# Second values spread ahead of the text's values, and other work between the product of y and z and the first maxima that read it

## The chip, the core and the metric

The kernel runs on one core of one Trainium2 chip. TensorE multiplies matrices (PE in the profile, with PEld for its loads of the stationary operand), VectorE (DVE) and ScalarE (ACT) work on the results, GpSimd (POOL) does elementwise work and issues gathers, and SyncE (SP) issues nearly all transfers. Each engine runs its own program in order; semaphores tie them. The metric is the device time of one execution in microseconds, as the median of several runs. All data are float32.

## The reference

Two batches of 2048 rows of 640 numbers (x) attend to a context of 128 tokens of 384 numbers, of which the last 4 are "ca" tokens and the first 124 are text.

```python
query = hidden_states @ Wq
keyt = enc @ Wk
valt = enc @ Wv
hs = _mha(query, keyt, valt)                       # text: 8 heads of 80, 124 keys
ca_q1 = jnp.einsum('btc,th->bch', ca, Wq_ca)
ca_q1 = ca_q1[:, indices, :]                       # 384 distinct rows, repeated to 2048
ca_hs1 = _mha(ca_q1, residual, residual)           # adapter, first attention: keys are x
ca_q2 = ca_hs1 @ Wq
ca_k2 = ca @ Wk_ca
ca_v2 = ca @ Wv_ca
ca_hs2 = _mha(ca_q2, ca_k2, ca_v2)                 # adapter, second attention: 4 keys
out = hs + ca_hs2
out = out @ Wout + b_out
out = out + residual
```

The text's attention is large and regular. The adapter's first attention runs over all 2048 rows of x with only 384 distinct queries, and its second has only four keys.

## The kernel before, in words

**Two kinds of work.** The *adapter* of a batch comes in two stages. In the first, x is taken in four blocks of 512 rows. `yz_block` (L756) multiplies a block's transposed rows with a small matrix `wyz` that holds the queries' four tokens by head and what the second attention's keys make of x (tile `pyz`), and ScalarE copies the two halves with a bias (L775, tile `yz`). `maxima` (L792) then multiplies yz with the ca tokens (tile `s`, L799), six times a block, each time 128 partitions of four banks, and VectorE takes the maximum of each (L806, tile `mx`). The tile `s` has one buffer of four PSUM banks, so each `s` product waits for the maximum of the one before. `y_rows` (L779) turns yz for later (`pt_y`). When the four blocks are through, `less_maxima` (L811) subtracts the maxima from the tokens. In the second stage, `contraction` (L825) multiplies again, ScalarE takes the exponential (tile `ea`), and TensorE contracts it with the turned rows (`acc`); at its end come the second attention with its four keys and its product with the values matrix `w2_sb` (`po2`, stored as o2, from which rows are added to the output by gathers on GpSimd).

The *text* comes in 16 units of two tiles of 128 rows: queries (`pq`, L936), scores (`sc`, L971), softmax on VectorE, ScalarE and GpSimd, a turn of the probabilities over device memory (`eb`, `kept`, `pT`, L1017 to L1039), values (`ph`) and the output product (`po`, L1049 on), which VectorE adds to x (`xo`). Tiles of the text that are ready before o2 is are stored and loaded again later (`early`, `xe`).

**What sets the order.** TensorE's order is the program's order. `TensorInOrder` (L18) keeps each matmul in program order and adds up an estimate of TensorE's time so far, `pe.us`. The main body writes the adapter's stages and fills what lies between them: `weave` (L1171) takes the pieces of a stage one by one, and after each lets `fill.run` issue other pieces until the stage's gap in estimated time is full. `Mix` (L98) chooses that other work from several lists (`Fill`, L66): `own` (the adapter's further stages, loads of x and setup), `text`, and `later`. A piece whose needs are not met is passed over, and where no list has one, `run` returns at once. A `Stage` may need a point in estimated time: `y_rows` may start only 1.0 us after its block's product (L1240, with `yz_at` from L776), and the transposes of a loaded block (`x_turn`, L741) 18 or 24 us after its load was issued. `fill.until` (L122) forces a list on until a stage is done. VectorE, ScalarE, GpSimd and SP serve their instructions in the order in which the scheduler puts them, which follows the program.

In the body, each block's maxima come right after `fill.until(done, ("yzT", b, sb))`, which ends with that block's product (L1269 and L1302).

**The values of the setup.** `setup_values` (L617) is one of the stages of `own`. It makes two things. The text's values: for each batch and half, three accumulating products (`pv`), which `spread` copies in three pieces into `vpad`. And the second values, those of the ca tokens: `by_groups` (tile `pvca`, copied to `vca`), then `groups_turned` (tile `pt_vca`, one transpose and four small products), then four instructions of VectorE that spread it into `blk_v`, and last `by_blocks` (tile `pw`), which multiplies it with the output matrix into `w2_sb`. Each `yield` is a point at which other work may be put in between. Tiles like `pv`, `pt_vca`, `pw`, `pyz` and `pq` share a pool of three PSUM banks in turn (`ps_m`); in the second batch's maxima a fourth bank joins.

Of the kernel before, what the change touches and what calls it, by code (L numbers as in the profile page):

```python
# [19 lines left out]
class TensorInOrder:  # L20
# [6 lines left out]
    def matmul(self, out, lhsT, rhs, **kw):  # L27
        ins = self.tc.nc.tensor.matmul(out, lhsT, rhs, **kw)  # L28
        self.tc.keep_in_program_order(ins)
        n = 1  # L30
        for size in rhs.shape[1:]:
            n *= size
        if min(lhsT.shape[0], lhsT.shape[1]) <= 32:
            self.us += (n / 1.2 + 97) / 2e3
        elif min(lhsT.shape[0], lhsT.shape[1]) <= 64:
            self.us += (n / 1.2 + 54) / 1e3
        else:
            self.us += 2 * max(n / 1.2, 109) / 1e3
# [139 lines left out]
def kernel(  # L178
# [39 lines left out]
    nc = tc.nc  # L218
    pe = TensorInOrder(tc)
    dve = VectorBehind(tc)  # L220
    B, S, H = x.shape
    NTOK, CAD = enc.shape[1], enc.shape[2]
    NK = NTOK - T
    D = H // HEADS
    NCH = H // P
    NCC = CAD // P
    NST = S // P
    NSB = S // 512
    HALF = H // 2
# [23 lines left out]
    matmul = pe.matmul  # L253
# [5 lines left out]
    def mm_tile(name, pool=None):  # L259
        if pool is None:  # L260
            pool = ps_turns[ps_turn[0] % len(ps_turns)]
            ps_turn[0] += 1
        return pool.tile([P, 512], F32, tag="mm", name=name)
# [4 lines left out]
    def evacuate(dst, src):  # L268

        turn[0] += 1  # L270
        if on[0][turn[0] % len(on[0])] == "A":
            nc.scalar.copy(dst, src)  # L272
        else:
            dve.tensor_copy(dst, src)
# [51 lines left out]
    vpad = [const.tile([P, HEADS, VH + 2 * VR], F32, name=f"vpad_{b}") for b in range(B)]  # L326
# [47 lines left out]
    w_c = {}  # L374
# [23 lines left out]
    ctxT = sp.tile([P, NCC, B, NTOK], F32, name="ctxT")  # L398
# [54 lines left out]
    def by_groups(name, rows, w):  # L453

        pg = mm_tile(name)
        for cc in range(NCC):
            for g in range(4):
                matmul(
                    pg[G * g : G * (g + 1), :D2], rows[:, cc, :], w[:, cc, D2 * g : D2 * (g + 1)],
                    start=(cc == 0), stop=(cc == NCC - 1), skip_group_check=True,  # L460
                )
        return pg

    def groups_turned(name, t, n):

        pt = mm_tile(name)
        transpose(pt[:, :P], t[:, :P], ident)
        for g in range(4):
            matmul(
                pt[R * g : R * (g + 1), P : P + n], t[:, P:], ident[:, G * g : G * g + n],  # L470
                start=True, stop=True, skip_group_check=True,
            )
        return pt[:, :P].rearrange("p (c k) -> p c k", c=4), pt[:, P : P + n]

    def by_blocks(name, *products):


        for to, rhs, first in products:
            for c in range(4):
                matmul(  # L480
                    to[G * c : G * (c + 1)], blk[name][:, 0, c, :], rhs(c),
                    start=first, stop=False, skip_group_check=True,
                )
        for to, rhs, _ in products:
            matmul(
                to, blk[name][:, 1].rearrange("p g k -> p (g k)"), rhs(4),
                start=False, stop=True, skip_group_check=True,
            )
# [128 lines left out]
    def setup_values():  # L617


        def spread(dst, src, u):  # L620

            s4 = src.rearrange("p (h d) -> p h d", h=4)
            d4 = dst[:, 4 * u : 4 * u + 4, :]
            evacuate(d4[:, :, :VH], s4[:, :, :VH])
            for j in range(2):
                evacuate(
                    d4.rearrange("p (g j) d -> p g j d", j=2)[
                        :, :, j, VH + VR * j : VH + VR * (j + 1)
                    ],
                    s4.rearrange("p (g j) d -> p g j d", j=2)[:, :, j, VH:],  # L630
                )

        pg = by_groups("pvca", caT, w_c["vca"])[:, :D2].rearrange("p (j d) -> p j d", j=2)
        vca = sp.tile([P, D2], F32, name="vca")
        evacuate(vca[:, :P].rearrange("p (j d) -> p j d", j=2), pg[:, :, :VH])
        evacuate(vca[:, P:].rearrange("p (j d) -> p j d", j=2), pg[:, :, VH:])
        yield
        for b in range(B):
            nc.gpsimd.memset(vpad[b], 0.0)
            for u in range(2):  # L640
                pv = mm_tile(f"pv_{b}_{u}")
                for cc in range(NCC):
                    matmul(
                        pv[:, :HALF],
                        ctxT[:, cc, b, :],
                        w_c["v"][:, cc, u * HALF : (u + 1) * HALF],
                        start=(cc == 0),
                        stop=(cc == NCC - 1),
                    )
                spread(vpad[b][:NK], pv[:NK, :HALF], u)  # L650
                yield
        most, rest = groups_turned("pt_vca", vca, B * T)
        for j in range(2):
            k0 = T * j
            dve.tensor_scalar(
                blk["v"][:, 0, :, : B * 2 * T].rearrange("p c (b k) -> p c b k", b=B)[
                    :, :, :, k0 : k0 + T
                ],
                most[:, :, : B * T].rearrange("p c (b t) -> p c b t", b=B),
                side2[:, j : j + 1], None, ALU.mult,  # L660
            )
        for b in range(B):
            n = 2 * T
            dve.tensor_tensor(
                blk["v"][:, 1, :, n * b : n * (b + 1)].rearrange("p g (j t) -> p g j t", j=2),
                rest[:, T * b : T * (b + 1)].rearrange("p (x y t) -> p x y t", x=1, y=1).to_broadcast(
                    [P, 4, 2, T]
                ),
                eighth.rearrange("p (g j x) -> p g j x", g=4, x=1).to_broadcast([P, 4, 2, T]),
                ALU.mult,  # L670
            )
        yield
        for u in range(2):
            cols = slice(u * HALF, (u + 1) * HALF)
            pw = mm_tile(f"pw2_{u}")[:, :HALF]
            by_blocks("v", (pw, lambda c: wout_sb[:, c, cols], True))
            evacuate(w2_sb[:N2, cols], pw[:N2])
        yield
# [9 lines left out]
    yz_at = {}  # L688
# [103 lines left out]
    def maxima(b, sq, mx, sb, gap):  # L792

        yz = yz_of[b, sb]
        for ct in range(NCC):
            for u in range(2):
                q4 = sq.tile([P, 4, 512], F32, tag="sq", name=f"s1_{b}_{sb}_{ct}_{u}")
                for g in range(4):
                    matmul(  # L799
                        q4[:, g, :],  # L800
                        ca0[G * g : G * (g + 1), u, ct * P : (ct + 1) * P],
                        yz[G * g : G * (g + 1), u, :],
                        start=True,
                        stop=True,
                    )
                dve.tensor_reduce(mx[:, ct, u, :, sb], q4, AX.X, ALU.max)  # L806
                yield gap
                if (ct, u) == (1, 0):
                    done.add(("half", b, sb))

    def less_maxima(b, mx):  # L811

        mt = pools["ea"].tile([P, NCC, 2, P], F32, tag="ea", name=f"mt_{b}")
        nc.gpsimd.memset(mt, 0.0)
        mt_cols = mt.rearrange("p a j (g k) -> p (a j) g k", k=32)[:, :, :, ONE]
        dve.tensor_reduce(mt_cols, mx.rearrange("p a j g s -> p (a j) g s"), AX.X, ALU.max)
        yield 1.0
        for j in range(2):
            pm = mm_tile(f"pm_{b}_{j}")
            for ct in range(NCC):  # L820
                transpose(pm[:, ct * P : (ct + 1) * P], mt[:, ct, j, :], ident)
            dve.tensor_tensor(ca0[:, j, :], ca0[:, j, :], pm[:, :CAD], ALU.subtract)
        yield 1.0
# [347 lines left out]
    def weave(main, fill, least=0.0):  # L1171


        due = 0.0
        for gap in main:
            due = fill.run(max(due + gap, min(gap, least)))
# [88 lines left out]
    fill = Mix(pe, (own, 1), (text, 1))  # L1265
    weave(setup_a2(), fill)
    own.parts[:0] = yz_stages(0, 0)
    for sb in range(NSB):
        fill.until(done, ("yzT", 0, sb))  # L1269
        weave(maxima(0, sq, mx_of[0], sb, 2.3), fill, 2.0)  # L1270
    fill.until(done, ("yz", 0, NSB - 1))
    fill.until(done, "values")
# [17 lines left out]
    fill = Mix(pe, (own, 1), (text, 1), (later, 1))  # L1290
# [9 lines left out]
    )  # L1300
    for sb in range(NSB):
        fill.until(done, ("yzT", 1, sb))  # L1302
        weave(maxima(1, sq, mx_of[1], sb, 4.8), fill, 2.0)
    weave(less_maxima(1, mx_of[1]), fill)
    fill.until(done, ("yz", 1, NSB - 1))
# [41 lines left out]
```

## Time and profile before

| what | value |
|---|---|
| three runs | 754.13, 750.59, 754.28 us; median 754.13 us |
| the profiled execution | 750.76 us |
| its span, first to last instruction | 749.1 us |
| granted clock of TensorE | 1.000 |
| TensorE idle in 0 to 150 us | 4.2 (first load), 2.6 (pw), 1.5 (yz), 1.0 (kpad), 0.2, 0.2 us |
| VectorE busy, 300 to 450 us | 109.6 of 150 us |
| moved by the DMA engines | 96.28 MB, 129 GB/s over the span |

A line of the profile's lists of groups and its timeline names the source line, the engine, the operation, and the tiles as out<-in; L28, L41 and L55 are the helpers through which all matmuls, transposes and most of VectorE's instructions go, so one tells them apart by tiles. One float32 matmul stands as two records. "x12" counts the records that were merged. In square brackets stands the time for which the engine had been idle, and what ended it; "issue" is idle time for which the profile shows no releaser. In the timeline the blocks and batches of a tile are not told apart; the times do that: the first batch's maxima run from 50 to 152 us, its contraction to 310, the second batch's maxima from 313 to 457 and its contraction to 603; after that the text is alone.

### The profile page before, as it was taken

The numbers are of one execution on the slowest core, as the hardware profiler recorded it, in microseconds if no ns is written. First come the engines' busy times: TensorE is split into PE (matmuls) and PEld (weight loads), VectorE is DVE, ScalarE is ACT, GpSimd is POOL, SyncE is SP. The second block draws the span as 40 slices with busy tenths as digits, with TensorE's granted clock in tenths as the row PEclk, the third lists the DMA queues.
The fourth block names the chain that finished last, engine by engine and source line by source line (L and its number), as shares of the span: only waits on it lengthen the run. The fifth ranks groups of instructions, "written<-read, shape, count | busy, mean of one in ns | idle before, by whom it ended". The sixth has DMA issues, their size and how long they took to land.

```text
span 749.1 us, 9397 instructions
## 1 busy us (share of the span) xinstructions
PE 727.0 (97%) x3809; PEld 372.2 (50%) x3809; DVE 373.3 (50%) x507; ACT 193.6 (26%) x239; POOL 133.4 (18%) x184
## 2 busy tenths in 40 slices
PE   7999989999989999999999999999999999999998
PEld 4553423343345446555445554434543556566765
DVE  2155736654264447488669586311440526345631
ACT  2221112033344433221112111443534311011100
POOL 7000000002021013225321221010010012631330
PEclk9999999999999999999999999999999999999999
DMA  9927240002824768298999294310920426985893
GB/s 294 169 40 120 34 38 1 0 1 92 127 96 83 187 106 186 88 244 175 187 268 230 60 201 114 116 41 4 190 61 18 127 91 191 237 219 153 214 245 95
DMA packets 147429, 96.28 MB, mean 129 GB/s; under 512 B 118133, under 2 KB 118965, under 8 KB 145338
## 3 DMA queue, kind: packets, MB, share of 16 engines
q1 hardware_dynamic: 142266, 85.10, 48.4%
q0 software_dynamic: 5120, 10.59, 8.1%
q8 instruction: 30, 0.49, 0.3%
q14 instruction: 13, 0.11, 0.1%
HBM read 63.81 MB, written 31.85 MB: 128 GB/s over the span
## 4 chain that ended last, share of the span: by engine, by line
PE 88%; DVE 5%; DMA 3%; issue 2%; ACT 1%; POOL 0%; SPq 0%; DVEq 0%; ACTq 0%; POOLq 0%
PE pq L28 24%; PE po L28 22%; PE s L28 13%; PE sc L28 10%; PE acc L28 6%; PE ph L28 5%; PE pyz L28 3%; DMA pT<-kept 2%; DVE mx L55 1%; PE pk L28 1%; ACT ea L856 1%; DVE m L55 1%; PE pt_y L41 1%; DVE p L55 1%; DVE xt L55 1%
## 5 line engine op out<-in xcount | busy, mean ns | idle before, releaser
L28 PE MATMUL po<-wout_sb,hsT 128*128 128x320 f32 x640 | 186.4, 438 | 1.5 <-DVE q L55 0.8
L28 PEld LDWEIGHTS po<-wout_sb,hsT 128*128 128x128 f32 x640 | 118.5, 190 | 70.5 <-issue 22.5
L28 PE MATMUL pq<-xt,wq_sb 128*128 128x512 f32 x320 | 151.9, 605 | 0.0
L55 DVE TENSOR_REDUCE mx<-s 128x4 f32<-128x2048 f32 x48 | 109.8, 2289 | 69.8 <-PE s L28 69.8
L856 ACT ACTIVATE ea<-s 128x1536 f32<-128x1536 f32 x64 | 92.7, 1448 | 109.3 <-PE s L28 109.2
L1014 POOL TENSOR_TENSOR p<-p,r 128x992 f32<-128x992 f32 x32 | 61.4, 1957 | 253.3 <-DVE r L55 253.3
L55 DVE TENSOR_TENSOR xo<-xo,po 128x320 f32<-128x320 f32 x64 | 31.0, 484 | 142.8 <-PE po L28 142.2
L28 PE MATMUL sc<-kpad,q 128*128 128x248 f32 x384 | 94.2, 385 | 0.1
L28 PEld LDWEIGHTS pq<-xt,wq_sb 128*128 128x128 f32 x320 | 57.0, 189 | 74.9 <-issue 68.4
L28 PEld LDWEIGHTS sc<-kpad,q 128*128 128x128 f32 x384 | 69.2, 189 | 32.4 <-issue 18.5
L55 DVE TENSOR_REDUCE m<-sc 128x4 f32<-128x496 f32 x64 | 42.2, 665 | 51.5 <-PE sc L28 51.4
L28 PE MATMUL s<-ca,yz 32*128 32x384 f32 x512 | 59.4, 533 | 2.5 <-ACT ea L856 2.5
L272 ACT COPY q<-pq 128x512 f32<-128x512 f32 x29 | 17.0, 585 | 163.5 <-PE pq L28 163.5
L28 PE MATMUL s<-yz,ca 32*128 32x512 f32 x384 | 54.7, 639 | 3.3 <-ACT yz L775 1.5
L999 ACT ACTIVATE p<-p 128x992 f32<-128x992 f32 x32 | 33.0, 1030 | 95.2 <-DVE p L55 92.6
L1109 POOL DMA_INDIRECT xo<-o,query x24 | 37.4, 1560 | 111.4 <-DMA xo<-in_x_dram 51.1
L28 PE MATMUL acc<-ea,y_sb 128*32 128x384 f32 x512 | 54.6, 498 | 0.2 <-ACT ea L856 0.2
L28 PE MATMUL ph<-pT,vpad 128*32 128x256 f32 (+1 forms) x512 | 50.0, 387 | 2.0 <-DVE hsT L55 1.8
L55 DVE TENSOR_TENSOR p<-sc,m 128x496 f32<-128x496 f32 x64 | 42.4, 669 | 1.5
L55 DVE STREAM_TRANSPOSE eb<-p 128x1024 f32<-128x1024 f32 x32 | 38.1, 1223 | 3.6 <-POOL p L1014 3.6
L28 PE MATMUL pq<-xt,wq 128*128 128x512 f32 x80 | 37.8, 601 | 0.0
L55 DVE TENSOR_REDUCE r<-p 128x8 f32<-128x992 f32 (+1 forms) x34 | 37.7, 1111 | 0.2
(142 smaller groups left out, 389.8 us busy)
## 6 DMA issues: line engine op xcount, KB each, us to landing
kept<-eb SPq DMA_DIRECT2D x16, 1024.0 KB, 5.1
pT<-kept SPq DMA_DIRECT2D x64, 256.0 KB, 5.5
xi<-in_x_dram SPq DMA_DIRECT2D x44, 256.0 KB, 5.0
xo<-in_x_dram SPq DMA_DIRECT2D x32, 320.0 KB, 5.6
out_dram<-xo SPq DMA_DIRECT2D x22, 320.0 KB, 3.3
xi<-in_x_dram SPq DMA_DIRECT2D x44, 64.0 KB, 4.8
early<-xo SPq DMA_DIRECT2D x8, 320.0 KB
xe<-early SPq DMA_DIRECT2D x8, 320.0 KB, 7.6
```

What stands on the lines that cost most here:

```text
L28: ins = self.tc.nc.tensor.matmul(out, lhsT, rhs, **kw)
L41: ins = self.tc.nc.tensor.transpose(out, in_, ident)
L55: self.last = getattr(self.tc.nc.vector, name)(*args, **kw).ins
L272: nc.scalar.copy(dst, src)
L856: nc.scalar.activation(e, q4[:, :, :CAD], AF.Exp, scale=SCALE)
L999: nc.scalar.activation(e[:, :, :NK], e[:, :, :NK], AF.Exp, scale=SCALE)
L1014: nc.gpsimd.tensor_tensor(et, et, r.unsqueeze(2).to_broadcast([P, HEADS, NK]), ALU.mult)
L1109: nc.gpsimd.indirect_dma_start(out=t, out_offset=None, in_=o2_of[b], in_offset=bass.IndirectOffsetOnAxis(ap=query[:, st : st + 1], axis=0) ...
```

## The change

In `setup_values` the turn of the second values and their spread into `blk_v` come before the text's values; both are the same instructions as before. In the body, after each block's product of y and z, `fill.run` is called once more, for as long as 1.2 us by the kernel's own count are not yet over since that product. The rest of the program is written as it was; since the fill then has other pieces at hand, what is put between later stages differs too.

```diff
@@ setup_values
         evacuate(vca[:, P:].rearrange("p (j d) -> p j d", j=2), pg[:, :, VH:])
         yield
-        for b in range(B):
-            nc.gpsimd.memset(vpad[b], 0.0)
-            for u in range(2):
-                pv = mm_tile(f"pv_{b}_{u}")
-                for cc in range(NCC):
-                    matmul(
-                        pv[:, :HALF],
-                        ctxT[:, cc, b, :],
-                        w_c["v"][:, cc, u * HALF : (u + 1) * HALF],
-                        start=(cc == 0),
-                        stop=(cc == NCC - 1),
-                    )
-                spread(vpad[b][:NK], pv[:NK, :HALF], u)
-                yield
         most, rest = groups_turned("pt_vca", vca, B * T)
...
                 ALU.mult,
             )
         yield
+        for b in range(B):
+            nc.gpsimd.memset(vpad[b], 0.0)
+            for u in range(2):
+                pv = mm_tile(f"pv_{b}_{u}")
+                for cc in range(NCC):
+                    matmul(
+                        pv[:, :HALF],
+                        ctxT[:, cc, b, :],
+                        w_c["v"][:, cc, u * HALF : (u + 1) * HALF],
+                        start=(cc == 0),
+                        stop=(cc == NCC - 1),
+                    )
+                spread(vpad[b][:NK], pv[:NK, :HALF], u)
+                yield
         for u in range(2):
             cols = slice(u * HALF, (u + 1) * HALF)
             pw = mm_tile(f"pw2_{u}")[:, :HALF]
@@ the first batch's maxima
     for sb in range(NSB):
         fill.until(done, ("yzT", 0, sb))
+        fill.run(yz_at[0, sb] + 1.2 - pe.us)
         weave(maxima(0, sq, mx_of[0], sb, 2.3), fill, 2.0)
@@ the second batch's maxima
     for sb in range(NSB):
         fill.until(done, ("yzT", 1, sb))
+        fill.run(yz_at[1, sb] + 1.2 - pe.us)
         weave(maxima(1, sq, mx_of[1], sb, 4.8), fill, 2.0)
```

## The prediction, made before the changed kernel ran

> **What bounds the kernel now.** I read the page first, then the list of waits of TensorE alone, then the timeline around the longest of them on TensorE and on VectorE, and last the list of what the SP queue issued.
>
> From the page (span, then busy time and share of each engine):
>
> ```profile
> span 749.1 us, 9397 instructions
> PE 727.0 (97%) x3809; PEld 372.2 (50%) x3809; DVE 373.3 (50%) x507; ACT 193.6 (26%) x239; POOL 133.4 (18%) x184
> ```
>
> TensorE is the path: 727.0 of 749.1 us, at a granted clock of 1.00 throughout. No edit of this change adds or removes a matmul, so it can only act on the 22.1 us in which TensorE idles. Who ended that idle time (the longest of the waits of TensorE: total, times, longest):
>
> ```profile
> PE pt_ctx L41 <- DMA ctx_sb<-in_ctx_dram: 4.2, 1, 4.2
> PE pw L28 <- DVE blk_v L55: 2.6, 1, 2.6
> PE s L28 <- ACT ea L856: 2.5, 4, 1.3
> PE ph L28 <- DVE hsT L55: 1.8, 1, 1.8
> PE s L28 <- ACT yz L775: 1.5, 2, 0.8
> ```
>
> 4.2 us is the first load, 2.5 and 1.8 us lie in the two contractions. What the two edits aim at is the wait of pw for blk_v (2.6 us) and the waits of the maxima's s for yz (1.5 us, and 0.82 us at 313.26 us that the profile could name only "issue", but that stands at the same place: s right behind pyz). Together 4.9 us: no forecast from these edits can go much beyond that. The timeline of TensorE in the stretch of the first edit (start, length, engine, line, operation; in brackets the idle time before it):
>
> ```profile
> 84.54 1.02 PE L28 MATMUL pvca<-w_vca,caT 128*32 128x160 f32 x24
> 85.50 1.14 PE L28 MATMUL s<-yz,ca 32*128 32x512 f32 x8
> 86.57 3.50 PE L28 MATMUL pv<-w_v,ctxT 128*128 128x320 f32 x12
> 90.28 1.14 PE L28 MATMUL s<-yz,ca 32*128 32x512 f32 x8 [0.22 <-DVE mx L55]
> 91.35 3.50 PE L28 MATMUL pv<-w_v,ctxT 128*128 128x320 f32 x12
> 94.78 1.14 PE L28 MATMUL s<-yz,ca 32*128 32x512 f32 x8
> 95.85 0.33 PE L41 MATMUL pt_vca<-ident,vca 128*128 128x128 f32 x1
> ...
> 98.96 2.89 PE L28 MATMUL pw<-wout_sb,blk_v 128*32 128x320 f32 x20 [2.60 <-DVE blk_v L55]
> 101.78 3.00 PE L28 MATMUL pyz<-xt,wyz 128*64 128x512 f32 x12
> 105.55 1.14 PE L28 MATMUL s<-yz,ca 32*128 32x512 f32 x8 [0.77 <-ACT yz L775]
> ```
>
> And VectorE, which serves in its program's order:
>
> ```profile
> 95.99 2.29 DVE L55 TENSOR_REDUCE mx<-s 128x4 f32<-128x2048 f32 x1 [2.21 <-PE s L28]
> 98.19 0.40 DVE L55 TENSOR_SCALAR blk_v<-pt_vca,side 128x32 f32<-128x32 f32 x2
> 98.51 0.28 DVE L55 TENSOR_TENSOR blk_v<-pt_vca,eighth 128x32 f32<-128x32 f32 x2
> ```
>
> The reader is to see that blk_v itself costs 0.6 us, but stands behind a maximum of 2.2 us, so that pw comes 2.6 us late.
>
> **Part one: the second values ahead.** Same instructions, moved. No transfer moves with them; the two memsets of vpad keep their place in POOL's order, and ACT's copies theirs. I walk through the new order with the durations above. pvca ends at 85.5, its copies on ACT at 85.98, s ends at 86.57; the turn of vca (0.5 us) then runs to 87.05 and waits for nothing. Two pv groups (3.43) end at 90.5. The maximum of the s before it is done at 90.2 (its row starts at 87.97, after the five transposes of x that start at 84.97), so the 0.22 us wait goes too, and s runs to 91.55. VectorE does blk_v behind that maximum, 90.2 to 90.8. The other pv groups end at 95.0, s at 96.05, and pw starts there instead of at 98.96: blk_v is five us old. pyz then starts at 98.9 instead of 101.78: **2.9 us less**. The cover of blk_v is the second s and the last two pv, 4.5 us on TensorE.
>
> [...] This pool has three banks. Before, the turn of vca was followed only by pw; now the third pv group takes its bank, and the bank is freed not by ACT's 0.55 us copies but by blk_v, behind a maximum. By the row blk_v ends at 90.8 and the third pv comes at 91.55: 0.75 us to spare, cost nothing. [...]
>
> **Part two: 1.2 us of other work after each pyz.** It inserts whatever fits by the kernel's own count. In the first batch's blocks 0 and 1 nothing fits (the next stages are not allowed yet): the new order of TensorE is the old one there, and the 0.77 us at 50.28 stays. In block 2 two matmuls of pq_4 (1.8 us) now stand between pyz and s; yz takes 1.26 us on ACT, so the **0.77 us** go. But the order after it moves too. On VectorE the five transposes of x's fourth block now stand ahead of the maximum of s_2_1_0 and not behind it:
>
> ```profile
> 116.37 3.07 DVE L55 STREAM_TRANSPOSE xt<-xi 128x512 f32<-128x512 f32 x5
> 119.36 2.25 DVE L55 TENSOR_REDUCE mx<-s 128x4 f32<-128x2048 f32 x1
> ```
>
> Summed with these rows from pyz at 98.9: s_2_0_0 103.65, s_2_0_1 107.5 and its maximum 108.7 to 110.9, transposes to 113.9, maximum of s_2_1_0 to 116.15. TensorE would start s_2_1_1 at 115.1 (pt_y 0.93, pq 1.81, s 1.07, pq 2.77 after 108.55), and s has one buffer. **About 1.1 us of new wait**, bounded by 0 and 2. Block 3 gets nothing in between and needs nothing. So the first batch gives 2.9 + 0.77 - 1.1 = **2.6 us**; from there to 305 us the order is the same and the gain is carried along, since the waits in it are for ACT and VectorE behind the same matmuls.
>
> In the second batch the order is mixed anew from 312 to 605 us, same work, and as many changes between kinds of matmul (454 before, 453 after), so no switching cost. Four places matter:
> - Behind the first pyz now stands sc (1.36 us): the 0.82 us at 313.26 goes. **0.8 us less.** The other three blocks had no such wait.
> - VectorE between s_0_2_0 and s_1_0_0: maximum 2.2, output sum 0.4, four transposes 2.5, two of eb 2.3, m and p 1.3: the first score bank is free 9.0 us after s_0_2_0, and TensorE asks for it after 8.0 (po 1.2, turns 0.93, sc 1.36, ph 1.0, s 1.07, sc 1.45, ph 1.0). 1.0 us against the 0.61 us that stood at 351.45 for the same queue: **0.4 us more**, bounded by -0.6 and +1.5.
> - The SP queue. The last transpose of the next block is no longer behind the first maximum, and the additions for the reloaded tiles on POOL no longer stand behind one that waits for po_7:
>
> ```profile
> 317.46 9.04 SPq L251 DMA_DIRECT2D xi<-in_x_dram  x8
> 356.11 7.42 SPq L251 DMA_DIRECT2D out_dram<-xe  x4
> 363.63 9.30 SPq L251 DMA_DIRECT2D xi<-in_x_dram  x8
> 381.81 17.79 SPq L251 DMA_DIRECT2D xi<-in_x_dram  x8
> ```
>
>   The first row waited 7.8 us for that transpose, the second 13.4 us for such an addition. Without them the first load starts at about 307 and the last of those stores at about 350, 10 us ahead. TensorE waited for no load in this stretch, so this is worth 0, but it pays for the next point: the load at 381.81 now stands behind one more store, out_dram<-xe.
> - In the second contraction the exponentials still stand behind the text's own (the 1.3 us in three waits there): 0, within 1 us either way. At 609.55 TensorE waited 0.79 us for a copy of q; two other products now stand in between: 0 to 0.8, I take **0.4 us less**.
>
> Sum: 2.6 + 0.8 - 0.4 + 0.4 = 3.4 us. The profiled execution took 750.76 us (span 749.1 and 1.7 around it), so it would take 747.4. That execution lies at the lower end of the runs (750.59 to 754.28, median 754.13); against the median the same 3.4 us give **750.7 us**.
>
> **Rivals.**
> - *No change.* The waits move instead of going: the 1.1 us in block 2 becomes 2, the mixing of the second batch costs 1.5 us where I say 0.4, q's wait stays. Then 3.4 - 0.9 - 1.1 - 0.4 = 1.0 us remain: 753.1. For it: VectorE is 73% busy from 300 to 450 us, and a maximum is due every 6 us. Against it: only 0.6 us of TensorE's idle there was owed to a maximum.
> - *More than the sum.* The second batch loses nothing at 351 and the earlier loads smooth the stretch from 350 to 400 us, where the DMA engines are fullest; or the run falls with the lower ones, as two of four did. 747.2 us.
> - *Slower.* The load of x for the text's next queries (381.81) now waits in SP for the store of the reloaded tile, whose addition was issued at 384.68 and needs some 6.7 us. If that addition comes no earlier, the load starts at 391.4, takes its 17.8 us again and lands 4.6 us later, at 413.8. VectorE reaches its transposes at 404.6 (405.2 before; 3.4 us of gain, and some 2.8 us of sums that now stand ahead of them), and waits 9.2 us with the next maximum behind it. TensorE has 1.3 us of room there, so it loses 7.9 us: 750.7 + 7.9 = 758.6. It decides from 3.4 us of TensorE's time on, a landing after 409.3. Against it: with SP and POOL 10 us ahead, the store is free at about 382, and even the slow 17.8 us land at 404.
>
> **How the numbers follow.** Forecast 0.50, no change 0.20, more than the sum 0.16, slower 0.14. 0.5% is 3.8 us, about what a measurement of this kernel tells from no change; the forecast's 3.4 us lies close to it, and the runs themselves lie 3.6 us apart, so of its 0.50 I put 0.30 to faster and 0.20 to the same, and 0.02 of the slower case to the same: faster 0.30 + 0.16 = 0.46, same 0.20 + 0.20 + 0.02 = 0.42, slower 0.12. The range goes from 745.5 (all 4.9 us and a run at the lower end: 745.9 from the profiled execution) to 755.5 (nothing gained, and the highest run with a little more); the forecast's own is 747 to 752.
>
> **What would show it.** In the profile after: no wait of pw for blk_v, and pyz of block 2 starting 14.4 us after pvca and not 17.2; s waiting for yz once, at 50 us, and no longer at 105 or 313; a new wait of s for mx of about 1 us near 115; TensorE's idle time near 18 us, busy time 727. Wrong would be: a wait of pv for blk_v; waits of s or sc for VectorE above 2 us between 335 and 350; VectorE waiting for xi near 400.

## The result: 1.0% faster, and the profile after

Seven runs of each kernel side by side: 754.28 us before (750.04 to 755.17), 745.51 us after (744.53 to 747.52). The ratio is 0.9898, with a 95% interval of 0.9872 to 0.9923. The forecast was 750.7 us: the sign is right, the size too small by 5 us.

The profiled execution after took 744.53 us, 6.2 us less than the one of before. Its page (span; busy time and share of TensorE, its weight loads and the other engines):

```profile
span 742.8 us, 9398 instructions
PE 725.1 (98%) x3809; PEld 371.3 (50%) x3809; DVE 376.3 (51%) x507; ACT 193.4 (26%) x239; POOL 133.1 (18%) x184
```

TensorE idles 17.7 us where it idled 22.1. The waits of TensorE in the changed kernel (total, times, longest):

```profile
PE pt_ctx L41 <- DMA ctx_sb<-in_ctx_dram: 4.4, 1, 4.4
PE s L28 <- ACT ea L856: 2.3, 3, 1.3
PE ph L28 <- DVE hsT L55: 1.8, 1, 1.8
PE pk L28 <- DVE kpad L55: 1.0, 2, 0.5
PE s L28 <- DVE mx L55: 1.0, 1, 1.0
PE pm L41 <- DVE ca L55: 0.9, 1, 0.9
PE sc L28 <- DVE p L55: 0.9, 1, 0.9
PE s L28 <- ACT yz L775: 0.8, 1, 0.8
```

The wait of pw for blk_v (2.6) is not there any more. The wait for yz stands once and not twice. New are s for mx and sc for p, 1.0 and 0.9 us. The timeline of TensorE in the stretch of the first edit and behind it (start, length, engine, line, operation, in brackets the idle time before):

```profile
83.66 1.02 PE L28 MATMUL pvca<-w_vca,caT 128*32 128x160 f32 x24
...
90.61 3.50 PE L28 MATMUL pv<-w_v,ctxT 128*128 128x320 f32 x12
94.04 1.14 PE L28 MATMUL s<-yz,ca 32*128 32x512 f32 x8
95.11 2.89 PE L28 MATMUL pw<-wout_sb,blk_v 128*32 128x320 f32 x20
97.94 3.00 PE L28 MATMUL pyz<-xt,wyz 128*64 128x512 f32 x12
100.86 1.98 PE L28 MATMUL pq<-xt,wq 128*128 128x512 f32 x4
102.78 1.14 PE L28 MATMUL s<-yz,ca 32*128 32x512 f32 x8
...
115.34 1.14 PE L28 MATMUL s<-yz,ca 32*128 32x512 f32 x8 [1.00 <-DVE mx L55]
116.41 3.00 PE L28 MATMUL pyz<-xt,wyz 128*64 128x512 f32 x12
```

pyz starts 14.28 us behind pvca, where it was 17.24. The third pv group (90.61) waits for nothing. The price stands at 115.34, where the forecast had put it.

TensorE idles 4.4 us less and is busy 1.9 us less, 6.3 us together; 0.9 of them lie ahead of any edit, since pvca comes at 83.66 and came at 84.54. That leaves about 5 us, not the 8.8 between the medians. The experiments were made to find the rest.

### The profile page after: what moved, and what is told of

It is laid out like the page before. It is cut to its first block, busy times and chain, and to the rows that moved or that the text cites. A ratio compares the mean times of both kernels' runs of the same rounds, so it can differ in the third digit from the quotient of the medians.

```text
span 742.8 us, 9398 instructions
## 1 busy us (share of the span) xinstructions
PE 725.1 (98%) x3809; PEld 371.3 (50%) x3809; DVE 376.3 (51%) x507; ACT 193.4 (26%) x239; POOL 133.1 (18%) x184
## 4 chain that ended last, share of the span: by engine, by line
PE 92%; DVE 4%; issue 1%; ACT 1%; DMA 0%; POOL 0%; DVEq 0%; ACTq 0%; POOLq 0%
PE po L28 24%; PE pq L28 24%; PE s L28 13%; PE sc L28 11%; PE acc L28 6%; PE ph L28 5%; PE pyz L28 3%; PE pk L28 1%; PE pv L28 1%; PE pt_y L41 1%; DVE m L55 1%; DVE p L55 1%; ACT ea L856 1%; DVE xt L55 1%; DVE mx L55 0%
```

## The experiments

Two theories went in. "Waits": the time follows the idle time of TensorE that the two edits remove. "Slack": executions of before lie on two levels, near 750 and near 755 us, because a transfer of x lands late near 405 us in some of them, and only the second batch's new order takes that away. The third theory, "clock", came out of the first four runs: behind a pause TensorE runs for a while at half speed (a granted clock of 0.50 for 6.8 us behind 2.60 us of wait in the next profile), so that the pause costs more than its length. The *granted clock* below is the share of TensorE's full speed that the profile reports.

### The kernel before once more

No edit; what was wanted was a profile at the upper level.

> The kernel before once more, for a profile of an execution at its upper level (754 to 755 us; the profiled one took 750.76). If the upper level is a late transfer (theory: slack), the profile shows some 3 to 4 us more of TensorE's idle time, in the second batch's maxima, behind VectorE waiting for xi near 405 us. If it is not (theory: waits), the idle time of TensorE stays at 22 us, give or take 1, and the extra lies ahead of the first matmul or is spread over its busy time.

It took 755.26 us, span 753.6, so it lies on the upper level. From 300 to 410 us TensorE is busy for 107.92 us, as in the lower execution of before, and nothing there waits for a load. "Slack" falls. What differs is TensorE's clock. Busy time of TensorE and its granted clock in four stretches, first of this execution, then of the one of before that the prediction was made from (start and end, length, busy time and records, clock, DMA share, GB/s):

```profile
92.00:95.40 3.40, 3.40 (x16) 1.00 1.13 157
95.40:99.00 3.60, 1.42 (x17) 1.00 1.13 128
99.00:105.80 6.80, 6.38 (x24) 0.50 0.01 2
105.80:110.00 4.20, 3.43 (x18) 1.00 0.00 0
```

```profile
95.40:99.00 3.60, 1.00 (x21) 1.00 1.46 122
99.00:105.80 6.80, 6.03 (x36) 1.00 0.03 4
```

And the timeline of TensorE there, in the execution at 755.26 us:

```profile
99.42 5.25 PE L28 MATMUL pw<-wout_sb,blk_v 128*32 128x320 f32 x20 [2.60 <-DMA xi<-in_x_dram]
104.60 3.59 PE L28 MATMUL pyz<-xt,wyz 128*64 128x512 f32 x12
...
220.44 1.08 PE L28 MATMUL ph<-pT,vpad 128*64 128x256 f32 x8 [1.83 <-DVE hsT L55]
```

The same 2.60 us of wait, but from 99.0 to 105.8 us TensorE's granted clock is 0.50: pw takes 5.25 us and not 2.89, pyz 3.59 and not 3.00. That is 2.95 us more, which no list of waits shows. Behind the 1.83 us wait of ph the clock is 0.50 again, from 221.9 to 225.3 us, and costs 1.4 us: ph starts 3.41 us later than in the lower execution (220.44 and 217.03), the s that waits for ea behind it 4.78 us later (259.89 and 255.11). Together the two drops cost 4.3 us; the spans of the two executions differ by 4.5 (0.5 us stand ahead of pw already, and 0.3 are made up at the end). (The releaser named for pw is another one here, but blk_v stands behind the same maximum.)

The mean granted clock of an execution counts such drops: 3.4 us at half are 0.0023 of 750 us, 6.8 us are 0.0045. The 25 runs of before that stand beside these experiments sort by it: four of the five at 1.000 took 749.8 to 750.7 us, five of the six at 0.997 or 0.998 took 751.5 to 752.0, six at 0.995 took 752.6 to 755.6, eight at 0.993 took 754.5 to 757.2. Two do not fit: one at 1.000 took 755.84 and one at 0.998 took 754.16 (the last section comes back to them).

### The parts alone

The values ahead alone:

```diff
+        most, rest = groups_turned("pt_vca", vca, B * T)
...
         for b in range(B):
             nc.gpsimd.memset(vpad[b], 0.0)
...
-        most, rest = groups_turned("pt_vca", vca, B * T)
```

> Part one alone: the second values ahead, no fill after the products. Both theories: the wait of pw for blk_v (2.6 us) and the one of s behind it (0.2) go and no other comes, 2.9 us less. Theory waits: 754.3 - 2.9 = 751.4. Theory slack (the rest of the gain is a late transfer that the second batch's new order no longer has): also 751.4, with runs as far apart as those of the kernel before, 4 to 5 us.

747.6 us, ratio 0.9938 (0.9914 to 0.9961). Of 12 executions one shows 0.995, one 0.997, ten 0.999 or more; the median of these ten is 747.4 us.

The fill alone, in both batches, with the values where they were:

```diff
         fill.until(done, ("yzT", 0, sb))
+        fill.run(yz_at[0, sb] + 1.2 - pe.us)
...
         fill.until(done, ("yzT", 1, sb))
+        fill.run(yz_at[1, sb] + 1.2 - pe.us)
```

> Part two alone: the fill after each product, the second values where they were. The wait for blk_v stays at 2.6 us. Theory waits: the two waits for yz (1.6 us) and the q wait (0.8) go, 1 us of wait for a maximum in block 2 may come: 1.5 to 2.5 us less, 752 to 753. Theory slack: the same and some 3 us more at the median, 748 to 750, with runs within 3 us of each other.

750.52 us, ratio 0.9959 (0.9937 to 0.9981). The pause of pw is still there, and five of 12 executions show 0.995 or less. Its profile, at 0.993, has the same two drops: 6.8 us from 100.74 and 3.4 us from 223.6.

The values, and the fill in the first batch only:

```diff
         fill.until(done, ("yzT", 0, sb))
+        fill.run(yz_at[0, sb] + 1.2 - pe.us)
```

> Part one, and the fill after the products in the first batch alone; the second batch's maxima keep the order before. Theory waits: 0.77 us of yz go and 1.0 us of a maximum come, so that it stands with part one alone, 751.2 to 751.6. Theory slack: the same median, with runs 4 to 5 us apart; only the second batch's fill brings the rest.

748.03 us, ratio 0.9926 (0.9899 to 0.9953); none of 8 executions at 0.995 or less.

All three medians lie 1.5 to 3.8 us under what "waits" had expected (751.4, 752 to 753, 751.2 to 751.6).

So the fill in the first batch gains nothing, and the one in the second batch gains 2.2 us (from 748.0 here to 745.8 for the changed kernel, at a clock of 0.999 or more). Where these come from shows in the waits of TensorE from the second batch's first pyz to the end, first with the fill in the first batch only, then in the changed kernel:

```profile
PE s L28 <- ACT ea L856: 1.3, 3, 0.5
PE s L28 <- issue: 0.8, 1, 0.8
PE po L28 <- DVE q L55: 0.8, 1, 0.8
PE s L28 <- DVE mx L55: 0.6, 1, 0.6
```

```profile
PE s L28 <- ACT ea L856: 1.0, 2, 0.5
PE sc L28 <- DVE p L55: 0.9, 1, 0.9
```

From that pyz to the end of the span it was 439.3 us with the fill in the first batch only and is 437.1 now. 1.7 us of the 2.2 are these waits; the other 0.5 are busy time.

### Useless work in the pause

If a pause costs more than its length, then work of no use, put into it, should make the kernel before faster. Four matmuls on pv's operands go into the bank of pw, which pw overwrites; the estimate `pe.us` is put back, so that the order of all else stays.

```diff
             pw = mm_tile(f"pw2_{u}")[:, :HALF]
+            if u == 0:
+                us = pe.us
+                for n in range(4):
+                    matmul(
+                        pw, ctxT[:, n % NCC, 0, :], w_c["v"][:, n % NCC, :HALF],
+                        start=True, stop=True,
+                    )
+                pe.us = us
             by_blocks("v",
```

> The kernel before, with four extra matmuls of no use (pv's operands, into the bank of pw, overwritten by pw itself; about 2.3 us) put into the 2.60 us in which TensorE waits for blk_v. Theory 'clock': the pause itself costs 2.6 us, and in some 6 of 10 executions it is also followed by 6.8 us at half the granted clock (pw 5.25 us instead of 2.89, pyz 3.59 instead of 3.00: 3 us more). With the pause filled the useless work costs nothing, the drop behind it goes, and the median falls from 753.2 to about 751 (750.3 where the clock is 1.000 throughout, 751.6 where it falls behind the later 1.83 us wait of ph), with no execution near 755. Theory 'waits' (only TensorE's idle time counts): pw starts where it started, so the median stays at 753.2. Rival 'power' (the clock falls because TensorE works hard, not because it rests): the executions at 755 stay or become more.

750.71 us (749.94 to 752.43) against 753.32 for the kernel before beside it, ratio 0.9963 (0.9942 to 0.9984). The timeline of TensorE of this kernel:

```profile
95.64 2.42 PE L28 MATMUL pw<-w_v,ctxT 128*128 128x320 f32 x8
98.05 2.89 PE L28 MATMUL pw<-wout_sb,blk_v 128*32 128x320 f32 x20
100.87 3.00 PE L28 MATMUL pyz<-xt,wyz 128*64 128x512 f32 x12
104.64 1.14 PE L28 MATMUL s<-yz,ca 32*128 32x512 f32 x8 [0.77 <-ACT yz L783]
```

TensorE does 2.4 us more and the kernel is 2.6 us faster. None of ten executions shows 0.995 or less (two show 0.998); of the 15 runs of before beside it seven do. "Waits" had said 753.2, and falls as the whole story; so does the thought that the clock falls because TensorE works hard.

### The pause put back into the changed kernel

Copies of no use on ScalarE, from pv's last bank to the bank of pw, hold pw back; nothing else changes its order. First seven of them, then thirteen.

```diff
             pw = mm_tile(f"pw2_{u}")[:, :HALF]
+            for n in range(7 if u == 0 else 0):
+                nc.scalar.copy(pw, pv[:, :HALF])
```

> The changed kernel with a pause put back in front of pw: seven copies on ScalarE of pv's bank into the bank of pw, of no use, behind the last copies of pv (some 0.41 us each by the copy of pw, 2.9 us from 94.7), so that pw starts at about 97.7 instead of 95.1 and everything else keeps its order. A pause of about 2.6 us. Theory 'waits': 745.6 + 2.6 = 748.2 in every execution. Theory 'clock': 748.2 where the clock stays at 1.000 and about 751.2 in the 4 to 7 of 10 where it shows 0.995, with pw at 5.25 us and pyz at 3.59; the median between 748.5 and 751.2.

> The same with thirteen copies: a pause of about 5.0 us, longer than a stretch of 3.41 us of the clock's grid wherever that falls. Theory 'waits': 745.6 + 5.0 = 750.6. Theory 'clock': the drop follows in every execution, none at 1.000, and costs about 3 us besides: 753.6.

Seven copies: 750.70 us (747.75 to 755.87), a wait of pw of 2.60 us again; five of 12 executions at 0.995 or less. The four at 0.999 or more, for which 748.2 had been expected, took 747.75, 750.11, 750.27 and 752.76 us. The last of them is the profiled one, and it had a slow start (last section); the other two were not profiled. Thirteen copies: 754.66 us (752.37 to 759.69), a wait of 5.25 us; eleven of 12 at 0.995 or less and one at 0.998, none at 1.000. The longer pause, in TensorE's timeline, with the granted clock of three stretches behind it (there the columns of all five engines come before the clock):

```profile
106.81 4.73 PE L28 MATMUL pw<-wout_sb,blk_v 128*32 128x320 f32 x20 [5.25 <-issue]
111.47 1.08 PE L28 MATMUL pyz<-xt,wyz 128*64 128x512 f32 x4
```

```profile
105.00:107.00 2.00, 0.19 (x4) 0.22 (x8) 0.00 (x0) 1.61 (x4) 0.00 (x0) 0.50 0.00 0
107.00:112.00 5.00, 5.00 (x24) 1.37 (x20) 0.00 (x0) 0.85 (x2) 0.35 (x1) 0.61 0.02 3
112.00:114.00 2.00, 2.00 (x12) 0.54 (x8) 0.00 (x0) 0.00 (x0) 0.51 (x3) 1.00 0.00 0
```

With the pause put back the drops are back, by the mean clock in some executions at 2.60 us and in all 12 at 5.25 us. In the profile the drop behind the longer pause costs 1.9 us and not the 3 expected: the s that waits 1.0 us for mx behind it starts 13.53 us later than in the changed kernel (128.87 and 115.34), of which 6.38 stand ahead of the pause already (pvca at 90.04 and 83.66) and 5.25 are the pause. The clock is 0.50 from 105 to 107 us already, while pw starts at 106.81: it falls while TensorE still waits, and part of the slow time costs nothing.

### A version with neither wait?

The fill in the second batch alone, with the values ahead, since the first batch's fill seemed to lose half a microsecond:

```diff
         fill.until(done, ("yzT", 0, sb))
-        fill.run(yz_at[0, sb] + 1.2 - pe.us)
```

> The values ahead, and other work behind pyz in the second batch alone (the first batch's order as with the values alone). 'Sum of parts': values alone 747.3 and both with the first batch 747.9 at a granted clock of 1.000 say that the first batch's fill loses 0.3 to 0.5 us (0.77 us of yz's wait gone, 1.0 us of mx's new); so this gives 745.0, half a microsecond under the changed kernel. If the first batch's fill is needed by what follows (later loads, order of the text), it ends at or above the changed kernel: 745.5 to 746.5.

The changed kernel beside it:

> The changed kernel itself beside the others on one chip. 745.5 us; theory 'clock': at most 2 of 10 executions under a clock of 0.998, since only the 1.83 us wait of ph is left to start a drop.

And, on top of e6, the 1.83 us wait of ph taken away by moving s and acc of the last row tile ahead of it:

```diff
                 last = e
-                yield gap
+                yield gap + {14: -1.2, 15: 1.2}.get(st, 0.0) * (b == j == 0)
```

> As e6, and in the first contraction one gap is 1.2 us shorter and the next 1.2 us longer, so that s and acc of the last row tile stand ahead of the ph that waits 1.83 us for hsT. Theory 'clock' and theory 'waits' both say that this wait goes: up to 1.8 us less, 743.2 if nothing else moves; 'clock' says besides that all executions stay at 1.000. The order of the text behind it is mixed anew, which may give back 0 to 2 us: 743.2 to 745.5.

e6 took 745.66 us (744.52 to 746.19), ratio 0.9887 (0.9866 to 0.9909); the changed kernel 746.16 (745.20 to 751.91), ratio 0.9918 (0.9887 to 0.9948). These two can't be told apart; the sum of parts would have had 745.0. e8 took 748.18 (744.30 to 749.42), ratio 0.9917 (0.9890 to 0.9943): no gain either. Its timeline of TensorE shows ph 0.20 us late at 214.71, and another wait in its place:

```profile
345.73 1.49 PE L28 MATMUL sc<-kpad,q 128*128 128x248 f32 x6 [2.19 <-DVE p L55]
```

The fill was mixed anew behind the edit, and what 214 us gained, 345 us took. Two of six executions still show 0.997 and 0.998; where those drops fall was not seen. No version here beats the changed kernel.

## Why the forecast was too small

- **In range by luck.** 745.51 us lies inside 745.5 to 755.5 by 0.01 us, and outside the forecast's own 747 to 752. The lower end stood for all 4.9 us of waits gone in a run at the lower end; what came instead was some 5 us, part of it from other places, and the median's move to the lower end.
- **Part one, 2.9 us: right, step by step.** pyz starts 2.96 us earlier behind pvca. The values alone take 747.4 us at full clock, 3.2 us under before's 750.6 (median of the 14 executions of before, of all that stand beside the experiments, that show 0.999 or more). The third pv takes the bank that blk_v frees: blk_v is done at 89.84 and that pv starts at 90.61, 0.77 us to spare where the sum had 0.75.
- **Part two, first batch: right, and worth nothing.** The 0.77 us went, 1.00 us of mx came (1.1 forecast). Alone it costs about half a microsecond, and leaving it out again was not to be told from noise.
- **Part two, second batch: right in place, too small in size.** The term was 0.8 - 0.4 + 0.4 = 0.8 us, and it measured 2.2. The 0.82 us behind the first pyz went as forecast. The price at the score bank is 0.87 for 0.61 us, 0.26 where 0.4 stood. The wait for the copy of q went whole, 0.8 and not 0.4, since two other products stood in between, as its step said. Two gains were not in the sum: 0.3 us of the waits for ea, and 0.5 us of busy time, which I had set to nothing because the number of changes between kinds of matmul was equal. What a change costs differs: in the changed kernel two records of pq take 0.86 us ahead of pt_wq (37.32 to 38.18) and 0.95 ahead of pa (38.73 to 39.68). Whether this makes up the 0.5 us was not shown.
- **"Against the median the same 3.4 us give 750.7": this step failed.** It took the 3.4 us between the profiled execution (750.76) and the median (754.13) as an offset that the change would leave. It isn't one. It is for the most part the price of half clock behind the pause that part one removes, and behind the later wait of ph (4.3 us together in e1). Of the 63 executions of before beside the experiments, 31 show 0.995 or less; with the pause put back or left in (e3, e9) 10 of 24; without the pause (the changed kernel in both its sets, e2, e4, e5, e6, e8) one of 54. So the median fell by about 5 us at full clock (750.6 to 745.8) and by most of the offset as well. How much of the offset is clock can't be divided exactly: the clocks of the seven runs of before beside the result are not on record, and of the 14 executions at 0.999 or more six took 753.1 to 756.2 us, for which slow starts may be the cause (my estimate; last section).
- **The profile before could not show it.** It was of an execution whose granted clock is given as 1.00 from end to end. In other executions, by the mean clock, the 2.60 us were followed by drops in about half (41 of 87 at 0.995 or less). The drops behind pw last 6.83 us and those behind ph 3.41, and the two begin 122.88 us apart in e1, 36 times 3.413 us. The execution that the prediction was made from had neither drop.
- **The rivals.** *No change* is out: the new waits are 1.0 and 0.9 us, not 2 and 1.5 more. *Slower* is out: SP issued the late store at 381.95 us and the load of x right behind it, at 382.40 to 392.4; VectorE comes to its transposes at 403.1 and doesn't wait. *More than the sum* has the nearest number, 747.2, but not for the reason it gave first: 345.94 us still pays 0.87. Its last half sentence, that the run falls with the lower ones, was the better one. What it lacked was that the change itself puts them there.

## What to carry to other kernels

Where a tuned kernel's runs lie on levels, look at the mean granted clock of each run before taking the distance as noise: a change may remove the level. Behind the TensorE pauses of 1.83, 2.60 and 5.25 us here, drops of the clock cost 1.4, 2.95 and 1.9 us more where they came, and in the 12 profiles none came behind waits of 1.3 us or less. So I would count such a pause at more than its length, and close it with useful work from elsewhere before closing several short ones of the same sum. Behind an edit of the fill, read the whole order after it: a wait removed in one place came back in another in the first batch here, and in e8.

## What the runs showed of the hardware besides

- **Between 1.8 and 2.6 us it depends on where the pause falls.** Where a profile shows both ends of a stretch of one clock, it lasts a whole multiple of 3.41 us: 3.41 for the drops behind ph in e1, e2, e3 and e10, 6.83 for those behind the pause of pw in e1, e3 and e10, 740.69 us, 217 times 3.413, at full clock in the lower execution of before, and 737.28, 216 times, in the changed kernel. Steps of 3.41 us, continued from such an end through the execution, are my estimate of a grid of windows. The busy time of TensorE in the windows around the pause of pw, in the lower execution of before, in e9 and in e1 (columns as in e1 above):

```profile
94.44:97.86 3.42, 1.92 (x19) 1.00 1.50 141
97.86:101.27 3.41, 2.31 (x19) 1.00 0.51 42
```

```profile
98.91:102.33 3.42, 1.84 (x11) 1.00 1.45 145
102.33:105.74 3.41, 2.39 (x19) 1.00 0.45 37
```

```profile
95.60:99.01 3.41, 1.22 (x17) 1.00 1.10 125
```

  In the first two an edge of this grid cuts the pause of 2.60 us, so that no window is idle for more than 1.6 us, and no drop follows. In e1 one window is idle for 2.2 us, in e3 for 2.1, in e10 for 2.5, and each time the clock falls at its end. So 2.1 to 2.5 idle us of a window's 3.41 were enough there. An estimate from these numbers: if the edge can fall anywhere, one window gets 2.1 us or more of a pause of 2.60 us in about half of the executions, and of one of 5.25 us in all. Of the 11 profiles with the 1.83 us wait of ph, four (e1, e2, e3, e10) show a drop behind it and seven none. In four of the seven the grid cuts the wait; in the other three (before, e4, e9) it lies whole in one window as in the four, and what decides there stays open. In none of the 12 profiles does a drop follow a wait of 1.3 us or less before TensorE's last matmul.
- **The start runs at half the pace as well, and for a varying time.** TensorE's first turns of x take 0.42 us each and later ones 0.27, and four of them take 0.85 us up to the next (7.87 to 8.72 in the lower execution of before) and later 0.44 (7.57 to 8.01 in the changed kernel). The trace's first record of the clock stands where this changes, at 7.3 us in the changed kernel and 9.1 in the execution of before; in e9 and e10 all turns of x, to 11.5 us, take 0.42 us or a little more. In the execution of before the profile's views count the clock as 1.00 from 4 to 9 us, where the turns take 0.42. So the mean clock does not show a slow start. In the profile of e9, at a clock of 1.000 and still 751.1 us long, late pieces of x hold TensorE up for 1.0 us near 6 to 8 us. The first 30 records of pq then take 15.3 us, and 13.1 us in the changed kernel:

```profile
L28 PE MATMUL pq<-xt,wq_sb 128*128 128x512 f32 x30 | 15.3, 675 | 0.0
```

```profile
L28 PE MATMUL pq<-xt,wq_sb 128*128 128x512 f32 x30 | 13.1, 596 | 0.0
```

  What follows stands 5.57 us later (p_kca at 27.82 and 22.25). In e10 the same 30 records take 16.2 us. Executions of several kernels at 1.000 that took 4 to 5 us more than the others (755.84 of before, 751.91 of the changed kernel) may have had such a start, an estimate; they were not profiled, and whether slow starts are as frequent in both kernels stays open. The 0.9 us between the profiles of before and after that lie ahead of any edit are there already when pq starts (10.07 and 9.18 us); half of the 1.8 us between their first clock records is as much.
